# Splitting three of proj_w's seven products once more, in an attention block on one Trainium2 core

## The chip, the cores and the metric

The kernel runs on one NeuronCore of one Trainium2 chip. The time is device microseconds of one execution, from the device's own clock. A core has five engines, each with its own instruction queue that runs in order: TensorE (PE in the profile, and PEld for its weight loads), VectorE (DVE), ScalarE (ACT), GpSimd (POOL) and SyncE (SP), which here issues the DMA transfers. TensorE writes its results to PSUM, which has eight banks of 2 KB per partition; a bank holds 512 fp32 values in each of 128 partitions. VectorE and ScalarE read PSUM; GpSimd works on SBUF alone.

## The reference

The reference is one cross-attention block in fp32 over x (8 sequences of 256 tokens, width 512) and a context of the same size, 16 heads of 32:

```python
x = layer_norm(hidden_states, ln1_w, ln1_b)
q, k, v = x @ q_w + q_b, enc @ k_w + k_b, enc @ v_w + v_b      # split in 16 heads
attn = softmax(where(mask, q k^T / sqrt(32), lowest))
hidden = (attn v) @ cproj_w + cproj_b + hidden_states
y = gelu(layer_norm(hidden, ln2_w, ln2_b) @ fc_w + fc_b)         # 512 -> 2048
out = hidden + y @ proj_w + proj_b                               # 2048 -> 512
```

## The kernel before, in words

Tokens are taken in four groups of 512 (`NG` = 4, `G` = 512). First comes the attention of all groups, then, from line 1101, a loop over the groups for the two large products: the fc stage (y by fc_w, gelu) and the proj stage (h by proj_w).

Matrix products use a Strassen scheme (Winograd's form): both operands are cut in quarters 11, 12, 21, 22, sums of quarters are made (`A_SUMS` for the left operand: s3, s2, s1, s4; `B_SUMS` for the right one: t1, t2, new 12, t4), and seven products of quarters take the place of eight. The seven are listed in `FC_ORDER`: 11 by 11, 12 by 21, s2 by t2, s3 by 12, s1 by t1, s4 by 22, 22 by t4.

The fc stage applies the scheme twice: `product(k)`, k from 0 to 6, is one of the seven outer products, and its function `sub` makes one of seven inner ones, four matmuls with 128 columns each. The inner products are added up in banks by the tags f1 (two buffers), f5 (two), f6 and f7, one bank for each inner partial product, read by VectorE (`add(V, ...)`, line 1122) or ScalarE (line 1277) while TensorE fills the next. What goes to h is combined on GpSimd (`add(GP, ...)` in `made`). The weights of outer product k (fc_w's quarter and its inner sums, 1.8 MB) stand in a ring of places: `load_w2` loads the next set into the place whose product has just ended. The places are k, q and c from the attention; place v holds y2, the inner sums of y for group 0, during group 0's fc stage, and line 1365 loads a set into it in group 0's proj stage, so that from then on the ring has four places. From group 1 on, y2 has a tile of its own, tag y2, with one buffer.

The proj stage applies the scheme once: `proj(bank, a, w, first, last)` makes one of seven products as 16 matmuls of 256 columns, with proj_w's quarters and sums (`pw`, made by VectorE in group 0, a few at a time, by `some_pw`). Their order on TensorE is 11 by 11, s3 by 12, 12 by 21, s2 by t2 (the operand h21 then holds s2), s4 by 22 (h12 holds s4), s1 by t1 (h11 holds s1), 22 by t4. h's sums s3, s2, s1, s4 are made by GpSimd (`sum_h`, four pieces each, in place over quarters that are no longer read). Between the first products TensorE turns the next group's y (`turn_next`), ScalarE evicts it, and VectorE makes its sums (`sum_up(V, ys[g + 1], ...)` and `split_y`, which writes the next y2). The result is added up in `ht` (tile resm): some of it by VectorE straight from PSUM (`o_add(V, ...)`), some by GpSimd from SBUF (`o_add(GP, ...)`); `store(0)` and `store(1)` send the two halves out.

All of this is written out in the order in which each engine runs it; each engine works through its list in order, and the tile framework adds the semaphore waits. It tracks SBUF by the ranges that instructions touch, and PSUM by bank.

Of the kernel before, what the change touches and what calls it, by code (L numbers as in the profile page):

```python
# [16 lines left out]
P = 128  # L17
# [5 lines left out]
def tile_xattn_block(  # L23
# [120 lines left out]
    def place(name, at):  # L144

        return Operand(wts.tile([P, 7, HC, S], F32, tag=f"w{at}", name=name))
# [23 lines left out]
    def rows_of(t):  # L170
        return t.rearrange("p i h s -> p i (h s)")
# [16 lines left out]
    def load_w2(at):  # L188

        if not w2_order:  # L190
            return
        g, k = w2_order.pop(0)
        t = rows_of(place(f"w2_{g}_{k}", at).t)
        n = FC_ORDER[k][0]
        if n in OWN:
            load_fc_quarter(lambda i: t[:, i], n, (0, 1, 3))
            nc.sync.dma_start(t[:, 2], w2_dram[QI[n]][:, 2])
            nc.sync.dma_start(t[:, 4:7], w2_dram[QI[n]][:, 4:7])
        else:
            nc.sync.dma_start(t, w2_dram[QI[n]])  # L200
        w2[g, k], w2_place[g, k] = t, at
# [14 lines left out]
    def sum_up(eng, x, table, *which):  # L216
        for i in which:
            to, a, b, op = table[i]
            eng.tensor_tensor(x[to], x[a], x[b], op)
# [75 lines left out]
    def split_y(g, t, *which):  # L295


        y2s[g] = t

        def quarter(n):  # L300
            if n in QUARTERS:
                return ys[g].t[:, :, int(n[0]) - 1, ts(int(n[1]) - 1, P)]
            return t[:, ("t1", "t2", "t4").index(n)]

        for i in which:
            to, a, b, op = B_SUMS[i]
            nc.vector.tensor_tensor(quarter(to), quarter(a), quarter(b), op)
# [15 lines left out]
    with ExitStack() as att:  # L323
# [671 lines left out]
        def run(pieces):  # L995
            for p in pieces:
                p()
# [103 lines left out]
    with ExitStack() as mlp:  # L1101
# [16 lines left out]
        def mm(ps, lhsT, rhs, first, last):  # L1118
            nc.tensor.matmul(ps, lhsT, rhs, start=first, stop=last, skip_group_check=True)  # L1119

        def add(eng, to, a, b, op=ALU.add):
            eng.tensor_tensor(to, a, b, op)  # L1122
# [23 lines left out]

        pw_sums = sum_pw()

        def some_pw(n):
            for f in zip(range(n), pw_sums):  # L1150
                pass
# [4 lines left out]
        for g in range(NG):  # L1156
# [15 lines left out]
                    [P, 2, S], F32, tag=f"f{n}", bufs=2 if n in (1, 5) else 1, name=f"{name}_{g}"  # L1172
                )

            def sum_h(which, q):

                x = {n: h[n][:, :, 2 * q : 2 * q + 2, :] for n in h}
                to, a, b, op = {
                    "s3": ("s3", "11", "21", ALU.subtract),
                    "s2": ("21", "22", "s3", ALU.subtract),  # L1180
                    "s1": ("11", "21", "11", ALU.add),
                    "s4": ("12", "12", "21", ALU.subtract),
                }[which]
                add(GP, x[to], x[a], x[b], op)

            def load_next():
                if g + 1 < NG:
# [47 lines left out]
            def product(k, *sums):  # L1235


                wt, yn = w2[g, k], QI[FC_ORDER[k][1]]
                bank = {}

                def y_of(n):
                    if n in QUARTERS:
                        return ys[g].t[:, yn, int(n[0]) - 1, ts(int(n[1]) - 1, P)]
                    return y2s[g][:, ("t1", "t2", "t4").index(n), yn, :]

                def sub(n, w, b, first, last):
                    if first:
                        bank[n] = bank_of(n, f"pf{n}_{k}").rearrange("p i (j s) -> p (i j) s", j=2)
                    for m in range(HF // 2):
                        mm(  # L1250
                            bank[n][:, m, :],
                            wt[:, QI[w], ts(m, P)],
                            y_of(b),
                            first and m == 0,
                            last,
                        )

                def u(n):
                    return us(n, f"u{n}_{k}").rearrange("p i (j s) -> p (i j) s", j=2)

                def made(cd, n, x):
                    some_gelus()
                    if k in (3, 4) and cd != "22":
                        norm_piece()
                    if sums[0][1] is None:
                        add(V, block(sums[0][0], cd), bank[n], x)
                        return

                    r = h["s3"][:, parts[0] % 4 // 2, parts[0] % 2 * HF // 2 :][:, : HF // 2]
                    parts[0] += 1  # L1270
                    add(V, r, bank[n], x)
                    for to, base in sums:
                        add(GP, block(to, cd), block(base, cd), r)

                sub(1, "11", "11", True, False)
                u1 = u(1)
                nc.scalar.copy(u1, bank[1])  # L1277
                sub(6, "s2", "t2", True, True)
                u2 = u(2)
                add(V, u2, bank[6], u1)  # L1280
                some_gelus()
                sub(7, "s3", "12", True, False)
                u3 = u(3)
                add(V, u3, bank[7], u2)
                some_gelus()
                sub(5, "21", "t1", True, False)
                made("22", 5, u3)
                sub(1, "12", "21", False, True)
                some_gelus()
                for to, base in sums:  # L1290
                    if base:
                        add(V, block(to, "11"), bank[1], block(base, "11"))
                    else:
                        nc.scalar.copy(block(to, "11"), bank[1])
                sub(7, "22", "t4", False, True)
                made("21", 7, u2)
                sub(5, "s4", "22", False, True)
                made("12", 5, u2)
                load_w2(w2_place[g, k])
# [5 lines left out]
            gelu("11", 0)  # L1305
            ht = residual(work, hid_dram[g], "resm", f"resm_{g}")
            product(2, ("21", "21"))
            product(3, ("12", "21"))
            if g == 0:
                load_pw("11", "12", "22")  # L1310
# [25 lines left out]
            def proj(bank, a, w, first, last, tiles=(0, 1)):  # L1336
                for i in tiles:
                    for p in range(HF):
                        mm(
                            bank[:, i, :] if last_7 is None or i == 0 or bank is not last_7[0] else last_7[1],  # L1340
                            h[a][:, i, p, :],
                            pw[w][:, p, :],
                            first and p == 0 and (i == 0 or last_7 is not None and bank is last_7[0]),
                            last and p == HF - 1,
                        )
# [11 lines left out]
            def o_add(eng, b, k, x):  # L1357
                o = out_quarter(b, k)
                add(eng, o, x, o)
# [1 line left out]
            u1, u2, u3 = (us(n, f"v{n}") for n in (1, 2, 3))  # L1361
            proj(bank[1], "11", "11", True, False)
            add(V, u1, bank[1], by_tiles(projb[:, HD2:]))
            if g == 0:
                load_w2("v")
            some_gelus(HF)
            normalise_next()
            for q in range(NQF):
                sum_h("s1", q)
            proj(bank[7], "s3", "12", True, False)  # L1370
            turn_next(0)
            turn_next(1)
            some_pw(4)
            proj(bank[1], "12", "21", False, True)
            o_add(V, 0, 0, bank[1])
            for q in range(NQF):
                sum_h("s4", q)
            turn_next(2)
            turn_next(3)
            some_pw(4)  # L1380
            proj(bank[6], "21", "t2", True, True)
            add(V, u2, bank[6], u1)
            if last_7 is None:
                add(V, u3, bank[7], u2)
            else:
# [3 lines left out]
                o_add(GP, b, k, u)  # L1389
            some_pw(4)  # L1390
            bank[3] = bank_of(1, "py3")
            proj(bank[3], "12", "22", True, True)
            o_add(V, 0, 1, bank[3])
            if g + 1 < NG:
                sum_up(V, ys[g + 1], B_SUMS, 0, 1, 2, 3)
            proj(bank[5], "11", "t1", True, True)
            o_add(V, 0, 1, bank[5])
            o_add(V, 1, 1, bank[5])
            store(0)
            if g + 1 < NG:  # L1400
                y2 = wpool.tile([P, 3, 7, P], F32, tag="y2", bufs=1, name=f"y2_{g + 1}")
                split_y(g + 1, y2, 0, 1, 2, 3)
                proj(bank[7], "22", "t4", False, True)
                o_add(V, 1, 0, bank[7])
                store(1)
            else:

                store(1, slice(HD2, D))
                for i in range(2):
                    proj(bank[7], "22", "t4", False, True, (i,))  # L1410
                    o = ht[:, 2 + i, :HD2]
                    add(V, o, last_7[1] if i else bank[7][:, 0, :], o)
                    store(1, slice(HD2), (i,))
# [41 lines left out]
```

## Time and profile before

| what | us |
|---|---|
| median of 3 runs | 727.32 (727.3 to 728.82) |
| the profiled execution's own time | 727.24 |
| its span, first to last instruction | 725.1 |
| fc stage of group 0, 1 | 347.3 to 391.0, 441.7 to 485.5 |
| proj stage of group 0, 1 | 391.0 to 441.7, 485.5 to 535.6 |
| fc and proj stage of group 3 | 629.5 to 673.1, 673.1 to the end |

The span and the lines of the profile are from one profiled execution; 2.1 us of its time lie outside the span. In a timeline line stand the start, the time, the engine, the source line, the operation, written tile <- read tiles, the count, and in brackets the engine's idle time before it with what ended it. In a group line stand, after the count, the busy time of all, the mean of one in ns, and the idle time before them. A matmul in fp32 is recorded as two records. Lines 1119 and 1122 are helpers (`mm` and `add`), so groups there are told apart by their tiles: pf is fc, py is proj.

### The profile page before, as it was taken

What the parts mean: (1) busy time and instruction counts of PE and PEld (TensorE: products, weight loads), DVE (VectorE), ACT (ScalarE), POOL (GpSimd) and SP (SyncE); (2) the same over time, 40 slices, a digit from 0 to 9 for tenths busy, and PEclk for the clock granted to TensorE, in tenths of its full rate; (3) what the DMA queues carried; (4) which work ended last, traced back from release to release, by engine and by line L of the source; (5) the groups of instructions that cost most, each with busy time, mean ns of one, the idle gap of its engine ahead of it and who ended that gap; (6) DMA issues with size and microseconds to landing.
All of it is one profiled execution on the core that took longest, in us unless ns stands there. A gap on an engine that the chain in (4) does not pass through costs nothing.

```text
span 725.1 us, 14073 instructions
## 1 busy us (share of the span) xinstructions
PE 719.1 (99%) x5109; PEld 627.6 (87%) x5109; DVE 416.9 (57%) x1056; ACT 321.8 (44%) x904; POOL 501.8 (69%) x451
## 2 busy tenths in 40 slices
PE   9999999999999999999999999999999999999998
PEld 7888777887888778777999889998899988999886
DVE  4676756675456657878588576770257701666111
ACT  2277798767777778871126200244002250021500
POOL 3857799986786999876569940599305895048970
PEclk9999999999999999999999999999999999999999
DMA  9616655598648775932799603981029820182001
GB/s 301 196 60 198 213 186 207 193 327 258 203 154 292 267 261 201 367 105 88 281 407 366 266 1 136 382 314 55 1 71 390 320 105 0 59 282 83 1 0 59
DMA packets 75380, 138.83 MB, mean 191 GB/s; under 512 B 6916, under 2 KB 45104, under 8 KB 72624
## 3 DMA queue, kind: packets, MB, share of 16 engines
q1 hardware_dynamic: 75056, 137.91, 54.0%
q8 instruction: 41, 0.67, 0.4%
q14 instruction: 27, 0.22, 0.1%
q0 software_dynamic: 256, 0.02, 0.0%
HBM read 104.36 MB, written 33.55 MB: 190 GB/s over the span
## 4 chain that ended last, share of the span: by engine, by line
PE 95%; ACT 1%; issue 1%; POOL 1%; DVE 1%; DMA 1%; SPq 0%; ACTq 0%; DVEq 0%; POOLq 0%
PE py L1119 25%; PE pf L1119 23%; PE ppt L699 8%; PE pv L441 7%; PE pqT L441 7%; PE po L441 6%; PE pkT L441 5%; PE s L646 5%; PE av L715 4%; PE pkT L538 2%; PE pxt L274 1%; PE pyt L274 1%; ACT h L1221 1%; PE pct L274 1%; DMA kw<-in_L_xattn_k_w_dram 1%
## 5 line engine op out<-in xcount | busy, mean ns | idle before, releaser
L1122 POOL TENSOR_TENSOR h<-h,hs 128x512 f32<-128x512 f32 x100 | 126.7, 1291 | 120.1 <-DVE hs L1122 119.7
L1119 PEld LDWEIGHTS pf<-y,w 128*128 128x128 f32 x1568 | 175.7, 192 | 0.2
L1119 PE MATMUL pf<-y,w 128*128 128x128 f32 x1568 | 175.7, 275 | 0.0
L688 POOL TENSOR_TENSOR pr<-pr,rsum 128x512 f32<-128x512 f32 x128 | 129.5, 1045 | 35.9 <-DVE rsum L686 24.2
L674 ACT ACTIVATE pr<-pr,nmax 128x256 f32<-128x256 f32 x256 | 127.6, 501 | 35.5 <-DVE nmax L664 35.3
L664 DVE CUSTOM_DVE_ANT_0 pr<-s,mb 128x256 f32<-128x256 f32 x256 | 93.5, 413 | 39.1 <-PE s L646 27.4
L1277 ACT COPY u<-pf 128x512 f32<-128x512 f32 x28 | 16.4, 585 | 200.0 <-PE pf L1119 200.0
L1119 PE MATMUL py<-pw,h 128*128 128x256 f32 x384 | 84.9, 379 | 0.0
L1119 PE MATMUL py<-pw_t,h 128*128 128x256 f32 x384 | 84.2, 379 | 0.0
L1119 PEld LDWEIGHTS py<-pw_t,h 128*128 128x128 f32 x384 | 72.7, 190 | 9.8
L1119 PEld LDWEIGHTS py<-pw,h 128*128 128x128 f32 x384 | 72.4, 190 | 9.6
L699 PEld LDWEIGHTS ppt<-ident,pr 128*128 128x128 f32 x512 | 57.3, 140 | 14.9 <-issue 5.2
L699 PE MATMUL ppt<-ident,pr 128*128 128x128 f32 x512 | 68.8, 276 | 0.3
L1122 DVE TENSOR_TENSOR resm<-py,resm 128x512 f32<-128x512 f32 (+1 forms) x21 | 13.6, 664 | 93.6 <-PE py L1119 93.6
L1122 DVE TENSOR_TENSOR hs<-pf,u 128x512 f32<-128x512 f32 x72 | 49.5, 689 | 13.3 <-PE pf L1119 12.1
L1221 ACT ACTIVATE h<-h,cols 128x256 f32<-128x256 f32 x128 | 52.0, 494 | 10.8 <-POOL h L1122 10.8
L1122 DVE TENSOR_TENSOR u<-pf,u 128x512 f32<-128x512 f32 x56 | 38.7, 691 | 28.7 <-PE pf L1119 24.6
L704 ACT COPY pt<-ppt 128x512 f32<-128x512 f32 x96 | 51.7, 573 | 7.1 <-PE ppt L699 7.1
L441 PE MATMUL pv<-vw,ctxT 128*128 128x256 f32 x224 | 52.4, 380 | 0.0
L441 PE MATMUL pqT<-xnT,qw 128*128 128x256 f32 x224 | 51.0, 379 | 0.0
L674 ACT ACTIVATION_READ_ACCUMULATOR pr<-pr,nmax 128x1 f32 x256 | 48.7, 190 | 0.0
L441 PEld LDWEIGHTS pqT<-xnT,qw 128*128 128x128 f32 x224 | 41.4, 190 | 5.0
(145 smaller groups left out, 1040.6 us busy)
## 6 DMA issues: line engine op xcount, KB each, us to landing
w<-w_dram SPq DMA_DIRECT2D x16, 1792.0 KB, 8.9
w<-in_L_xattn_fc_w_dram SPq DMA_DIRECT2D x36, 256.0 KB, 6.1
w<-w_dram SPq DMA_DIRECT2D x12, 768.0 KB, 7.5
ctx<-in_ctx_dram SPq DMA_DIRECT2D x16, 256.0 KB, 5.0
x<-in_x_dram SPq DMA_DIRECT2D x16, 256.0 KB, 4.0
v_dram<-st_v SPq DMA_DIRECT2D x16, 256.0 KB, 2.3
v<-v_dram SPq DMA_DIRECT2D x16, 256.0 KB, 4.7
resx<-in_x_dram SPq DMA_DIRECT2D x16, 256.0 KB, 4.6
```

The lines of the kernel that those rows point to most:

```text
L274: nc.tensor.transpose(ps[:, ts(t, P)], xt[:, ts(c, P)], ident)
L441: nc.tensor.matmul(bank[n][:, i, :], l[:, c, ts(i, P)], r[:, c, :], start=first and i == 0 and c == 0, stop=last and c == HC - 1, skip_gro ...
L646: nc.tensor.matmul(banks[j][:, i, :], qT[j * HD : (j + 1) * HD, b * S + i * P : b * S + (i + 1) * P], kT[j * HD : (j + 1) * HD, b * SK : ( ...
L664: nc.vector.tensor_tensor_reduce(pr[:, j, i, :], banks[j][:, i, :], mbias[g][1][:, b, :], scale=-SCALE, scalar=FLT_MAX, op0=ALU.add, op1=A ...
L674: nc.scalar.activation(pr[:, j, i, :], pr[:, j, i, :], AF.Exp, bias=nmax[:, j, i : i + 1], scale=-1.0, accum_out=sums[:, j, i : i + 1],)
L688: nc.gpsimd.tensor_tensor(pr[:, j], pr[:, j], rsum[:, j, :, None].to_broadcast([P, NQ, SK]), ALU.mult,)
L699: nc.tensor.transpose(ps[:, kc, ts(i, P)], probs[n][:, j, i, ts(kc, P)], ident)
L704: nc.scalar.copy(pt, ps)
L715: nc.tensor.matmul(av[j * HD : (j + 1) * HD, :], vs[g, hg][:, b * NK + kc, ts(j, HD)], pts[n, j][:, kc, :], start=(kc == 0), stop=(kc == N ...
L1119: nc.tensor.matmul(ps, lhsT, rhs, start=first, stop=last, skip_group_check=True)
L1122: eng.tensor_tensor(to, a, b, op)
L1221: nc.scalar.activation(h[n][:, :, p, :], h[n][:, :, p, :], AF.Gelu_apprx_tanh, bias=col(c_fcb, half * HF + p), scale=1.0,)
```

## The change

In groups 1 to 3 (`deep`), three of the seven proj products, s2 by t2, s1 by t1 and s4 by 22, are each made by `deep_proj`: the operands are cut in quarters again and seven inner products of four matmuls with 128 columns are made. Their results go to four quarters of one bank (`ps[:, 0]` to `ps[:, 3]`), and each is read, by ScalarE or VectorE, into 128-column pieces x1, x2, x3 or of the result r.

- h's inner sums are made by VectorE: `h_blocks`, four adds for each of the three operands, into a tile `hsum` that takes turns with y2 in the one buffer of tag y2, and into pieces of s3's tile (`free`). Two of the four pieces of h's s4 sum go from GpSimd to VectorE.
- The inner sums of the three weights are made once on VectorE (`p2_sums`: t1 and 22 in group 0, t2 in group 1's fc stage). t2's and 22's share a place, and are stored to DRAM and loaded again by SP in each group (`p2_load`).
- The results of s1 by t1 and s4 by 22 are added to `ht` by GpSimd instead of VectorE.
- s1 by t1 comes ahead of s4 by 22 in all groups; the next group's y sums come one at a time within s1 by t1.
- Place v holds p2 and the pieces x1 to x3; `load_w2("v")` is gone, so the ring for fc_w keeps three places.

```diff
+        p2, p2_at = [], {"t2": 0, "22": 0, "t1": 3}
+        p2_dram = {n: tc.dram_tile([P, 3 * S * 2], F32, name=f"p2_dram_{n}") for n in ("t2", "22")}
+        def p2_place(n):
+            if not p2:
+                p2.append(rows_of(place("p2", "v").t).rearrange("p i s -> p (i s)"))
+            return p2[0][:, p2_at[n] * 2 * S :][:, : 3 * 2 * S]
...
+        def p2_sums(n):
+            sum_up(V, pw_blocks(n), B_SUMS, 0, 1, 2, 3)
+            if n != "t1":
+                nc.sync.dma_start(p2_dram[n], p2_place(n))
+        def p2_load(n):
+            nc.sync.dma_start(p2_place(n), p2_dram[n])
...
             product(2, ("21", "21"))
+            if g == 1:
+                p2_sums("t2")
...
-            if g == 0:
-                load_w2("v")
...
+            deep = g > 0
+            if deep:
+                hsum = wpool.tile([P, 3, 7, P], F32, tag="y2", bufs=1, name=f"hsum_{g}")
...
+            def h_blocks(n, s3, s2, s4, s1=None):
...
+                for to, a, b, op in A_SUMS:
+                    add(V, x["s1" if to == "21" else to], x[a], x[b], op)
+                return x
+            def deep_proj(ps, x, w, r, others=()):
+                others = iter(others)
+                ps, y = ps.rearrange("p i (j s) -> p (i j) s", j=2), pw_blocks(w)
+                x1, x2, x3 = (p2[0][:, 6 * 2 * S :][:, ts(i, P)] for i in range(3))
+                r = r.rearrange("p c s -> p (c s)").rearrange("p (b s) -> p b s", b=4)
+                def sub(i, a, b, first=False):
+                    for c in range(HF // 2):
+                        mm(ps[:, i], x[a][:, c, :], y[b][:, c, :], first and c == 0, c + 1 == HF // 2)
+                sub(0, "11", "11", True)
+                nc.scalar.copy(x1, ps[:, 0])
+                sub(1, "s2", "t2")
+                add(V, x2, ps[:, 1], x1)
+                sub(2, "s3", "12")
+                add(V, x3, ps[:, 2], x2)
+                sub(3, "s1", "t1")
+                add(V, r[:, 3], ps[:, 3], x3)
+                run(next(others, ()))
+                sub(0, "12", "21")
+                nc.scalar.copy(r[:, 0], ps[:, 0])
+                sub(2, "22", "t4")
+                add(V, r[:, 2], ps[:, 2], x2)
+                run(next(others, ()))
+                sub(3, "s4", "22")
+                add(V, r[:, 1], ps[:, 3], x2)
+                run(next(others, ()))
...
+            if deep:
+                x_s2 = h_blocks("21", *(hsum[:, i] for i in range(4)))
             proj(bank[1], "12", "21", False, True)
             o_add(V, 0, 0, bank[1])
+            if deep:
+                x_s1 = h_blocks("11", free(0), free(1), free(2))
             for q in range(NQF):
-                sum_h("s4", q)
+                sum_h("s4", q, V if deep and q % 2 else GP)
...
-            proj(bank[6], "21", "t2", True, True)
-            add(V, u2, bank[6], u1)
+            if deep:
+                deep_proj(bank[6], x_s2, "t2", hsum[:, 4])
+                p2_load("22")
+                add(V, u2, as_tiles(hsum[:, 4]), u1)
+            else:
+                proj(bank[6], "21", "t2", True, True)
+                add(V, u2, bank[6], u1)
...
-            proj(bank[3], "12", "22", True, True)
-            o_add(V, 0, 1, bank[3])
-            if g + 1 < NG:
+            if deep:
+                x_s4 = h_blocks("12", hsum[:, 0], hsum[:, 1], hsum[:, 3])
+                y_sums = []
+                if g + 1 < NG:
+                    y_sums = [lambda i=i: sum_up(V, ys[g + 1], B_SUMS, i) for i in range(4)]
+                deep_proj(bank[5], x_s1, "t1", free(3), (y_sums[:1], y_sums[1:2], y_sums[2:]))
+                for b in range(2):
+                    o_add(GP, b, 1, as_tiles(free(3)))
+                deep_proj(bank[3], x_s4, "22", hsum[:, 4])
+                if g + 1 < NG:
+                    p2_load("t2")
+                o_add(GP, 0, 1, as_tiles(hsum[:, 4]))
+            else:
+                proj(bank[5], "11", "t1", True, True)
+                o_add(V, 0, 1, bank[5])
+                o_add(V, 1, 1, bank[5])
+                p2_sums("t1")
+                proj(bank[3], "12", "22", True, True)
+                o_add(V, 0, 1, bank[3])
                 sum_up(V, ys[g + 1], B_SUMS, 0, 1, 2, 3)
...
                 split_y(g + 1, y2, 0, 1, 2, 3)
+                if not deep:
+                    p2_sums("22")
```

In the prediction, S2, S1 and S4 are the three products s2 by t2, s1 by t1 and s4 by 22, a part is one of the seven inner products of a split one, and a read is the ACT or VectorE instruction that takes a part's result from the bank.

More of the change, by code (lines that the diff above doesn't have):

```diff
@@ L1147, in tile_xattn_block, with pw_blocks @@
         pw_sums = sum_pw()
+        p2, p2_at = [], {"t2": 0, "22": 0, "t1": 3}
[4 more added lines that the diff above has]
+            return p2[0][:, p2_at[n] * 2 * S :][:, : 3 * 2 * S]
+        def pw_blocks(n):
+            x = {
+                f"{k + 1}{j + 1}": pw[n][:, k * HF // 2 : (k + 1) * HF // 2, ts(j, P)]
+                for k in range(2)
+                for j in range(2)
+            }
+            t = p2_place(n).rearrange("p (n c s) -> p n c s", n=3, c=HF // 2)
+            return x | {m: t[:, i] for i, m in enumerate(("t1", "t2", "t4"))}
+        def p2_sums(n):
[4 more added lines that the diff above has]
+            nc.sync.dma_start(p2_place(n), p2_dram[n])
         def some_pw(n):
@@ L1173, in bank_of, with sum_h @@
                 )
-            def sum_h(which, q):
+            def sum_h(which, q, eng=GP):
                 x = {n: h[n][:, :, 2 * q : 2 * q + 2, :] for n in h}
@@ L1183, in sum_h @@
                 }[which]
-                add(GP, x[to], x[a], x[b], op)
+                add(eng, x[to], x[a], x[b], op)
             def load_next():
@@ L1369, in tile_xattn_block, with free, as_tiles @@
                 sum_h("s1", q)
+            deep = g > 0
+            if deep:
+                hsum = wpool.tile([P, 3, 7, P], F32, tag="y2", bufs=1, name=f"hsum_{g}")
+                hsum = hsum.rearrange("p t n s -> p (t n s)")[:, : 5 * 2 * S]
+                hsum = hsum.rearrange("p (b c s) -> p b c s", b=5, c=HF // 2)
+            def free(i):
+                return h["s3"][:, i // 2, i % 2 * HF // 2 :][:, : HF // 2]
+            def h_blocks(n, s3, s2, s4, s1=None):
+                x = {
+                    f"{i + 1}{k + 1}": h[n][:, i, k * HF // 2 : (k + 1) * HF // 2, :]
+                    for i in range(2)
+                    for k in range(2)
+                }
+                x |= {"s3": s3, "s2": s2, "s4": s4, "s1": x["21"] if s1 is None else s1}
+                for to, a, b, op in A_SUMS:
[26 more added lines that the diff above has]
+                run(next(others, ()))
+            def as_tiles(r):
+                return r.rearrange("p c s -> p (c s)").rearrange("p (i s) -> p i s", i=2)
             proj(bank[7], "s3", "12", True, False)
@@ L1391, in tile_xattn_block @@
             bank[3] = bank_of(1, "py3")
-            proj(bank[3], "12", "22", True, True)
-            o_add(V, 0, 1, bank[3])
-            if g + 1 < NG:
+            if deep:
[17 more added lines that the diff above has]
+                o_add(V, 0, 1, bank[3])
                 sum_up(V, ys[g + 1], B_SUMS, 0, 1, 2, 3)
-            proj(bank[5], "11", "t1", True, True)
-            o_add(V, 0, 1, bank[5])
-            o_add(V, 1, 1, bank[5])
             store(0)
```

## The prediction

> **What bounds the kernel now.** I read the page's first two parts, then the chain that ended last, then the costliest groups.
>
> ```profile
> PE 719.1 (99%) x5109; PEld 627.6 (87%) x5109; DVE 416.9 (57%) x1056; ACT 321.8 (44%) x904; POOL 501.8 (69%) x451
> PEclk9999999999999999999999999999999999999999
> PE 95%; ACT 1%; issue 1%; POOL 1%; DVE 1%; DMA 1%; SPq 0%; ACTq 0%; DVEq 0%; POOLq 0%
> ```
>
> TensorE is busy 99% of the span at full granted clock, and the chain is TensorE for 95% of it. So two things move the time: TensorE's own work, and any wait that opens a gap in it. The timeline of TensorE in group 1 prices the work:
>
> ```profile
> 347.26 43.93 PE L1119 MATMUL pf<-y,w 128*128 128x128 f32 x392
> ...
> 492.39 7.07 PE L1119 MATMUL py<-pw,hs 128*128 128x256 f32 x32
> 499.30 1.04 PE L274 MATMUL pyt<-ident,hm 128*128 128x128 f32 x8
> ```
>
> A proj_w product is 32 records (16 matmuls, two passes each) of 256 columns; the next thing starts 499.30 - 492.39 = 6.91 us later, 0.216 us each. The fc stage runs 392 records of 128 columns in 43.93 us, 0.112 us each, with no gap. It can, because each of its partial products has a bank to itself while the one before is read. The timeline of VectorE there shows the reader's delay:
>
> ```profile
> 639.48 0.69 DVE L1122 TENSOR_TENSOR hs<-pf,u 128x512 f32<-128x512 f32 x1 [0.20 <-PE pf L1119]
> 640.37 0.69 DVE L1122 TENSOR_TENSOR h<-pf,h 128x512 f32<-128x512 f32 x1 [0.20 <-PE pf L1119]
> ```
>
> An eight-record part ends every 0.893 us, and the read starts 0.20 us after the slot in which the next part has already begun.
>
> **The change, part by part.**
>
> **Work taken from TensorE.** A split product is 7 parts of 4 matmuls, 56 records of 128 columns: 56 x 0.1117 = 6.25 us for 6.91. Three products in three groups: 9 x 0.66 = 5.9 us saved. That is all there is to win.
>
> **Waits put into TensorE.** All seven parts of a split product go to quarters of one bank. I looked up in the built program what each part's first matmul waits for. Of each of the six parts after the first, it is the ACT or VectorE instruction that reads the part before it, though that instruction reads another quarter of the bank. So TensorE stops, the quarter is read, TensorE starts again: 6 x 9 = 54 gaps. No row shows a 128x128 read of PSUM, so I take it from its neighbours, by lines kept apart by shape:
>
> ```profile
> L1122 DVE TENSOR_TENSOR resm<-py,resm 128x512 f32<-128x512 f32 x19 | 12.8, 690 | 88.4 <-PE py L1119 88.4
> L1122 DVE TENSOR_TENSOR resm<-py,resm 128x256 f32<-128x256 f32 x2 | 0.8, 424 | 5.2 <-PE py L1119 5.2
> L369 ACT COPY ctxT<-pct 128x256 f32<-128x256 f32 x6 | 2.2, 359 | 0.0
> L564 ACT COPY cols<-ps_cols 128x44 f32<-128x44 f32 x1 | 0.2, 195 | 2.2 <-PE ps_cols L563 2.2
> ```
>
> 690 ns for 512 columns and 424 for 256 make 1.04 ns a column, so about 290 ns for 128; ACT, between 195 and 359, about 250. The way back is in one place of the attention's end, where a matmul waits for VectorE:
>
> ```profile
> 333.87 0.69 DVE L629 TENSOR_TENSOR st_o<-po,po_u 128x512 f32<-128x512 f32 x1 [0.37 <-PE po L441]
> 334.69 1.38 PEld L441 LDWEIGHTS po<-cw,att 128*128 128x128 f32 x7 [0.41 <-DVE st_o L629]
> ```
>
> The read ends at 334.56, the weight load starts 0.13 us later (other places: 0.05 to 0.11), and the matmul behind it is recorded 0.10 us longer than its like, its own weight load no longer hidden. A gap is thus 0.20 + 0.29 + 0.09 + 0.10 = 0.68 us. Bounds: 0.20 + 0.195 + 0.05 + 0.10 = 0.55, and 0.25 + 0.42 + 0.13 + 0.10 = 0.90. I take 0.68, since both durations lie on a line through two measured sizes. 54 x 0.68 = 36.7 us (30 to 49).
>
> [...]
>
> **VectorE late for the first read.** VectorE gets 12 adds per group to make the blocks' sums, half of h's s4 sums, and 15 reads of parts. Adds of SBUF by SBUF meet POOL's. The timelines of group 0 (both at work) and group 1 (one at a time):
>
> ```profile
> 398.75 6.10 DVE L1122 TENSOR_TENSOR pw_t<-pw,pw 128x512 f32<-128x512 f32 x4
> 522.65 2.68 DVE L219 TENSOR_TENSOR y<-y 128x512 f32<-128x512 f32 x4
> 394.18 6.78 POOL L1122 TENSOR_TENSOR hs<-h,h 128x512 f32<-128x512 f32 x4
> 488.20 4.96 POOL L1122 TENSOR_TENSOR hs<-h,h 128x512 f32<-128x512 f32 x4
> 500.48 9.88 POOL L1122 TENSOR_TENSOR h<-h,h 128x512 f32<-128x512 f32 x8
> ```
>
> Alone an add takes 0.67 us on VectorE and 1.24 on POOL. Together about 1.7 on each: they take turns. Adds that read PSUM stay at 0.69. On group 1's clock:
> - S2 (h21 by t2) would start at 507.95, behind the read of bank 1 at 507.3 to 508.0 on VectorE. In VectorE's queue behind that read stand S1's four sums and two halves of s4. POOL's s1 and s4 sums (500.48 on) are themselves pushed back some 2 us by S2's four sums, so the first two adds take turns with POOL: 1.5 + 1.8 + 0.6 + 0.6 + 2 x 0.65 = 5.8, until 513.8. The second part is ready for its read at 507.95 + 0.9 + 0.68 + 0.9 + 0.2 = 510.6. TensorE waits 3.2 us more.
> - S1 follows. VectorE: last read of S2 (0.5 after S2's end), u2 and u3 (1.35), S4's four sums, three of them in turn with POOL's three adds to resm (5.5): 7.3. Due 2.7 after S2's end: 4.6 late.
> - S4: two sums of y against POOL's two adds: 1.4 late, in groups 1 and 2 only.
> Sum 3 x 7.8 + 2 x 1.4 = 26.2 us. If VectorE never met POOL it would be 1.4 + 1.8 = 3.2 a group, 9.6; if every add took 1.75, some 34. I take 26.2, since POOL's queue places its adds there.
>
> **Sums of the weights.** Four adds for t1 in group 0 lie under the 6.9 us of product 12 by 22. Four for 22, queued behind split_y, delay the first reads of group 1's fc: about 1.5 us. Four for t2, after product 2 of group 1's fc, run against POOL, some 5.5 us ahead of product 3's reads: TensorE waits about 3. Together 4.5 (0 to 7).
>
> **Costed at nothing.** The ring of three places: in group 0's fc there were three places already (the fourth held y2), each load beside as much other traffic, and the first fence shows 392 records in 43.93 us without a gap. Cover gone, each late load would stop TensorE for its lateness. Stores and loads of p2 (0.79 MB each): SP waits for S2's or S4's end before each load; behind the first stand only the second and the stores of out, and the first has all of S1 to land, the second the next 22 by t4 and fc. The deep product leaves resm to POOL, so store(0) waits for one more POOL add (1.24); the last product covers it, and split_y too: it ends some 6 us after S4, where TensorE has 6.9 of 22 by t4 and 0.9 more. The other order of S1 and S4 in group 0: t1 is made by 420.1 and would be read from 421.0.
>
> **Sum.** -5.9 + 36.7 + 26.2 + 4.5 = +61.5. The profiled execution took 727.24 us (span 725.1; median of the runs 727.32, the same): 788.7, say 789.
>
> **The rivals.**
> - *Late reads hidden.* VectorE and POOL hardly meet: -5.9 + 36.7 + 9.6 + 1 = +41, 769. Against it stands POOL's unbroken line from 488 to 510.
> - *The clock falls in the gaps.* If TensorE ran at half rate in the nine products, 9 x 6.25 = +56 more, 845. Against it, the clock row, but that has no such gaps. [...]
> - *fc_w late.* A landing at the longest seen, 16.0 us, against the 12.5 us that two products leave, is 3.5 us; at two loads a group, +21, 810.
> - *Other side: faster.* The reads lie in the shadow of the next part after all, so that the gaps vanish: 727.2 - 5.9 = 721, or with the weights' sums 726. It decides where a gap with all that comes late stays under 5.9 / 54 = 0.11 us. The read alone is over 0.19 us; only a wait list that I misread could do it.
>
> **How the numbers follow.** Forecast 0.75 (775 to 803), late reads hidden 0.14, clock 0.04, fc_w 0.04, faster 0.03. The lower bounds together give 727.2 - 5.9 + 30 + 9.6 = 761, the upper ones 727.2 - 5.9 + 49 + 34 + 7 = 811; range 760 to 811. About 0.2% (1.5 us) is what a measurement of this kernel tells from no change. Slower 0.96, same 0.01, faster 0.03.
>
> **What would show it.** Each split product should take 10.5 us or more on TensorE, with six gaps near 0.7 us named after ACT or VectorE; one gap of 3 to 5 us in S2 and in S1 of each group; TensorE's share near 92%; group 0's proj stage as long as before. Parts following each other at 0.89 us would prove me wrong, as would gaps named after DMA.

## The result, and the profile after

The changed kernel takes 801.39 us (median of 4 runs, 799.72 to 804.39) against 727.48 us for the kernel before: 1.102 times as long, with an interval of 1.098 to 1.106. The forecast was 789 us in a range of 760 to 811. The profiled execution of the changed kernel is the longest of the four, 804.39 us, with a span of 802.6; it is 77.15 us above the profiled execution of before, and this is the amount to be explained.

The page of the changed kernel, busy shares and granted clock, and the shares of the chain that ended last:

```profile
PE 748.6 (93%) x5325; PEld 651.9 (81%) x5325; DVE 484.0 (60%) x1146; ACT 326.4 (41%) x922; POOL 517.2 (64%) x454
PEclk9999999999999999999999999968999979999889
PE 77%; DVE 8%; issue 7%; POOL 4%; ACT 2%; DMA 1%; SPq 0%; DVEq 0%; POOLq 0%; ACTq 0%
```

TensorE's share fell from 99% to 93% and the chain now runs through VectorE and GpSimd too. The clock row, all nines before, has a 6, an 8, a 7 and two more 8s, all of them late in the span. TensorE's own busy time *rose* from 719.1 to 748.6 us although a split product holds less work (28 matmuls of 128 columns for 16 of 256). Two things are counted as busy that aren't work: records at half clock are longer (eight take 2.02 to 2.08 us in the timeline below), and eight records that stand alone between two gaps are counted from the start of the first to the end of the last (1.16 us, where eight within a stream take 0.893).

What TensorE waited for from 385 us to the end (total, times, longest):

```profile
PE py L1119 <- DVE p L1122: 29.0, 18, 4.7
...
PE pf L1119 <- DVE resm L1122: 2.1, 1, 2.1
PE pf L1119 <- DVE u L1122: 1.7, 1, 1.7
```

Waits named after the reads of parts, as forecast, and two in fc of group 1 (pf). No row is named after a DMA. The timeline of TensorE in group 1, from S2's third part on, then S1 and S4:

```profile
520.79 1.16 PE L1119 MATMUL py<-pw_t,hsum 128*128 128x128 f32 x8 [2.83 <-DVE p L1122]
522.34 2.02 PE L1119 MATMUL py<-p,hsum 128*128 128x128 f32 x8 [0.39 <-DVE p L1122]
...
532.23 1.16 PE L1119 MATMUL py<-p,hs 128*128 128x128 f32 x8 [0.41 <-ACT p L1435]
538.07 2.08 PE L1119 MATMUL py<-pw_t,hs 128*128 128x128 f32 x8 [4.68 <-DVE p L1122]
...
549.84 1.06 PE L1119 MATMUL py<-pw,h 128*128 128x128 f32 x8
551.30 1.16 PE L1119 MATMUL py<-p,hsum 128*128 128x128 f32 x8 [0.41 <-ACT p L1435]
552.90 1.16 PE L1119 MATMUL py<-pw,hsum 128*128 128x128 f32 x8 [0.44 <-DVE p L1122]
```

Three things stand in these lines. S4, from 549.84, is the plain case: parts start 1.46 to 1.64 us apart instead of 0.893, each after some 0.4 us of idle time. S2 and S1 each have one long wait on top, 2.83 and 4.68 us. And some parts after such a wait take 2.02 to 2.08 us for the eight records that take 1.06 to 1.16 elsewhere. Windows over S2, S1 and S4 of group 1, and last over the middle of S1 alone (start and end, length, busy time of PE, PEld, DVE, ACT and POOL, granted clock, DMA share, GB/s):

```profile
515.39:530.76 15.37, 10.51 (x58) 9.08 (x57) 6.08 (x11) 1.63 (x4) 2.06 (x2) 0.78 0.02 3
530.76:549.84 19.08, 12.27 (x59) 10.74 (x58) 8.92 (x13) 0.53 (x2) 4.60 (x3) 0.64 0.10 40
549.84:560.17 10.33, 7.81 (x58) 6.69 (x57) 3.69 (x7) 0.53 (x2) 3.22 (x2) 1.00 0.05 8
...
536.10:549.80 13.70, 10.02 (x40) 8.87 (x41) 3.98 (x8) 0.27 (x1) 0.56 (x1) 0.50 0.00 1
```

The clock, third from the end of a line, is 0.78, 0.64 and 1.00, and 0.50 in the stretch from 536.10 to 549.80. A split product without a long wait takes 10.33 us, in all three groups, and one with it 15 to 19. The nine together take 132.13 us; at 10.33 each they would be 93.0. Of the 39.2 us above that, the six long waits, each less the 0.45 us that a gap there has anyway, are 21.5 (in group 1: 2.38 in S2, 4.23 in S1); the other 17.6 are parts inside the stretches at half clock, most of which start 2.2 to 2.6 us apart.

VectorE's timeline shows what the long waits wait for. The first two lines are from S2 of group 1, the other three from S1; below them is GpSimd's line beside S1:

```profile
516.43 1.57 DVE L1122 TENSOR_TENSOR hs<-h,hs 128x512 f32<-128x512 f32 x1
...
520.45 0.28 DVE L1122 TENSOR_TENSOR p<-py,p 128x128 f32<-128x128 f32 x1
...
535.58 1.63 DVE L1122 TENSOR_TENSOR h<-hsum,h 128x512 f32<-128x512 f32 x1
537.13 0.68 DVE L1122 TENSOR_TENSOR hsum<-h,hsum 128x512 f32<-128x512 f32 x1
537.74 0.28 DVE L1122 TENSOR_TENSOR p<-py,p 128x128 f32<-128x128 f32 x1
```
```profile
532.06 4.60 POOL L1122 TENSOR_TENSOR resm<-v,resm 128x512 f32<-128x512 f32 x3 [14.60 <-DVE v L1122]
```

The 0.28 us read that TensorE waits for stands last, behind the sums for the *next* split product and, in S2, two pieces of s4. While GpSimd adds (532.06 to 536.66), an add on VectorE takes up to 1.63 us; once GpSimd is through, 0.68.

TensorE's timeline in fc of group 1:

```profile
447.20 23.33 PE L1119 MATMUL pf<-y,w 128*128 128x128 f32 x192 [2.08 <-DVE resm L1122]
472.27 20.81 PE L1119 MATMUL pf<-y,w 128*128 128x128 f32 x184 [1.74 <-DVE u L1122]
```

VectorE makes the sums of 22 (443.93 to 446.54) and of t2 (466.78 to 470.81), and then, until just before these waits end, the reads that had to queue behind them. A stretch of 3.4 us at half clock follows the first wait (447.3 to 450.7, clock 0.50). The stage takes 49.75 us for 43.77.

So the whole difference, from the profiled executions: -5.9 of TensorE work, +36.7 for the 54 gaps, +21.5 late reads, +17.6 half clock in the split products, +6.0 in group 1's fc, and +1.5 by which fc of group 0 already began later (348.73 against 347.26): 77.4 for 77.15. The last of these is in the attention, which the change doesn't touch; in a profile of the kernel before with a ring of three places (below), whose attention is the same too, that stage begins at 348.64.

### The profile page after: what moved, and what is told of

The parts are those of the page before. It is cut to its first block, busy times and chain, and to the rows that moved or that the text cites. A ratio compares the mean times of both kernels' runs of the same rounds, so it can differ in the third digit from the quotient of the medians.

```text
span 802.6 us, 14693 instructions
## 1 busy us (share of the span) xinstructions
PE 748.6 (93%) x5325; PEld 651.9 (81%) x5325; DVE 484.0 (60%) x1146; ACT 326.4 (41%) x922; POOL 517.2 (64%) x454
## 4 chain that ended last, share of the span: by engine, by line
PE 77%; DVE 8%; issue 7%; POOL 4%; ACT 2%; DMA 1%; SPq 0%; DVEq 0%; POOLq 0%; ACTq 0%
PE pf L1119 20%; PE py L1119 16%; PE ppt L699 7%; PE pv L441 6%; PE pqT L441 6%; PE po L441 5%; PE pkT L441 5%; PE s L646 4%; PE av L715 4%; POOL h L1122 2%; DVE hs L1122 2%; PE pkT L538 2%; DVE hsum L1122 2%; DMA hm<-hid_dram 1%; POOL resm L1122 1%
## 5 line engine op out<-in xcount | busy, mean ns | idle before, releaser
L1122 POOL TENSOR_TENSOR h<-h,hs 128x512 f32<-128x512 f32 x100 | 128.5, 1308 | 103.0 <-DVE hs L1122 101.3
L1119 PE MATMUL pf<-y,w 128*128 128x128 f32 x1568 | 177.9, 277 | 3.8 <-DVE resm L1122 2.1
L1119 PEld LDWEIGHTS pf<-y,w 128*128 128x128 f32 x1568 | 177.5, 193 | 4.4 <-DVE resm L1122 2.3
L664 DVE CUSTOM_DVE_ANT_0 pr<-s,mb 128x256 f32<-128x256 f32 x256 | 93.6, 414 | 39.1 <-PE s L646 27.4
L1119 PE MATMUL py<-pw,h 128*128 128x256 f32 (+1 forms) x336 | 70.2, 365 | 1.4 <-DVE hsum L1122 1.4
L1119 PEld LDWEIGHTS py<-pw,h 128*128 128x128 f32 x336 | 60.0, 190 | 9.0 <-issue 1.9
L1119 PE MATMUL py<-pw_t,h 128*128 128x256 f32 (+1 forms) x288 | 60.2, 369 | 2.9 <-DVE hsum L1122 1.4
L1119 PEld LDWEIGHTS py<-pw_t,h 128*128 128x128 f32 x288 | 52.5, 212 | 9.3 <-issue 4.4
L1122 DVE TENSOR_TENSOR hs<-pf,u 128x512 f32<-128x512 f32 x72 | 49.6, 689 | 12.9 <-PE pf L1119 11.6
L1122 POOL TENSOR_TENSOR resm<-v,resm 128x512 f32<-128x512 f32 x12 | 18.4, 1562 | 44.3 <-DVE v L1122 44.3
```

The source lines that it names most:

```text
L664: nc.vector.tensor_tensor_reduce(pr[:, j, i, :], banks[j][:, i, :], mbias[g][1][:, b, :], scale=-SCALE, scalar=FLT_MAX, op0=ALU.add, op1=A ...
```

## The experiments

My theory, after the traces: two separate faults cost nearly everything, the common bank (54 gaps) and the sums ahead of the first reads (long waits); the lowered clock is a follow-on of the long waits and not of the short gaps; the ring of three places, the stores and loads of p2, and the order cost nothing. The rivals: the short gaps lower the clock too; the reads are late from VectorE's load as such, wherever its sums stand; the transfers or the ring cost something that the gaps hide. The first two experiments remove one fault each, the third both.

**Two banks.** The parts alternate between the old bank and a second one, so that a part's neighbours in time lie elsewhere; the last two parts change places for it.

```diff
-                ps, y = ps.rearrange("p i (j s) -> p (i j) s", j=2), pw_blocks(w)
+                ps = ps.rearrange("p i (j s) -> p (i j) s", j=2)
+                odd = odd_bank.rearrange("p (b s) -> p b s", b=4)
+                ps = [ps[:, 0], odd[:, 1], ps[:, 2], odd[:, 3]]
...
-                sub(1, "s2", "t2")
+                sub(1, "s2", "t2", True)
...
+                sub(3, "s4", "22")
+                add(V, r[:, 1], ps[3], x2)
+                run(next(others, ()))
                 sub(2, "22", "t4")
...
+                odd_bank = ps_m.tile([P, G], F32, tag="mm", name=f"odd_{g}")
```

> The parts of a split product go to two banks in turn (a free bank of the transposes takes parts 1 and 3), and the last two parts change places so that neighbours never share a bank; nothing else changes. Theory (three costs: 54 gaps of 0.68 us, VectorE late for the first read of S2 and S1, clock halved after those long gaps): the short gaps go, 801.4 - 36.7 = 764.7, within 3 us; two gaps of 2 to 5 us a group stay, now ahead of part 3, and the mean granted clock stays at 0.97. Rival (VectorE's queue is the real bound, the short gaps only show it): the waits move and the time stays within 10 us of 801.

Measured: 763.41 us (761.38 to 764.93), 1.0476 times before (1.0459 to 1.0494). The waits and the timeline of TensorE with two banks:

```profile
PE odd L1119 <- DVE p L1122: 24.9, 8, 4.5
...
```
```profile
518.43 1.16 PE L1119 MATMUL odd<-p,hsum 128*128 128x128 f32 x8 [2.57 <-DVE p L1122]
519.42 1.06 PE L1119 MATMUL py<-pw_t,h 128*128 128x128 f32 x8
520.32 1.06 PE L1119 MATMUL odd<-pw_t,hsum 128*128 128x128 f32 x8
...
529.49 2.08 PE L1119 MATMUL odd<-p,h 128*128 128x128 f32 x8 [4.54 <-DVE p L1122]
531.35 1.91 PE L1119 MATMUL py<-pw_t,h 128*128 128x128 f32 x8
```

The short gaps are gone: parts follow each other at 0.89 us. The long waits have stayed, 24.9 us of eight waits against 24.2 of six in the changed kernel, and so has the half clock after most of them, but not after the 2.57 us of the first line. The medians are 801.4 - 763.4 = 38.0 us apart, the two spans 39.5. By the starts of the parts the nine products take 95.0 us for 132.1, 37.1 less: the short gaps' 36.7 are gone, the late reads cost 27.2 for 21.5, as they come due earlier without the gaps, and the half clock 11.6 for 17.6. Fc of group 1 is 1.6 us shorter, because no half clock follows its first wait here, and the rest, some 0.7, lies ahead of it. The mean clock is 0.980, a little over the 0.97 of the expectation.

**Sums later.** One bank as in the change, but the sums for S1 stand behind the reads within S2, those for S4 within S1, those of y within S4, and all of s4 is back on GpSimd.

```diff
-                x_s1 = h_blocks("11", free(0), free(1), free(2))
+                x_s1, sums_s1 = h_blocks("11", free(0), free(1), free(2))
...
-                deep_proj(bank[6], x_s2, "t2", hsum[:, 4])
+                deep_proj(bank[6], x_s2, "t2", hsum[:, 4], (sums_s1[:2], sums_s1[2:]))
...
-                deep_proj(bank[3], x_s4, "22", hsum[:, 4])
+                deep_proj(bank[3], x_s4, "22", hsum[:, 4], (y_sums[:2], y_sums[2:]))
```

> One bank as in the changed kernel, but VectorE makes S1's block sums between the reads of S2, S4's between the reads of S1, the y sums between the reads of S4, and GpSimd makes all of s4 again; the work is the same. Theory: the long gaps go, and with them the clock's falls: before 727.5 - 5.9 saved + 36.7 short gaps + 7 weight sums = 765, mean clock 0.99 or more. Rival A (the many short gaps lower the clock): clock stays near 0.97 and the time at 780 or more. Rival B (the adds only move the lateness to other reads): over 775, with gaps over 1 us ahead of later parts.

Measured: 764.84 us (762.7 to 765.47), 1.0500 (1.0483 to 1.0517). The waits with the sums later, and a window over the three split products of group 1:

```profile
PE py L1119 <- DVE p L1122: 7.5, 18, 0.5
PE py L1119 <- DVE hsum L1122: 5.6, 12, 0.5
...
```
```profile
515.15:546.18 31.03, 23.45 (x171) 20.11 (x169) 12.87 (x29) 2.70 (x8) 10.29 (x9) 1.00 0.10 29
```

The row that had 29.0 us in 18 waits has 7.5 in the same 18; the row below it is the same to the tenth in both kernels. VectorE makes as many sums for the split products as before, so in S1, where nothing else was moved, it was their place in its queue and not its load. In S2 two changes go together: the sums' place and the two pieces of s4 that went back to GpSimd (1.29 us on VectorE in the changed kernel, of the 2.4 to 4.1 us there). All 54 gaps are still there, and the clock is 1.00 over the split products of every group; the one stretch at half clock (0.998 over the span) lies in fc of group 1. So these 54 gaps of 0.35 to 0.48 us do not lower it, and the rival which has the short gaps lower the clock falls. Late reads and the clock together cost 801.4 - 764.8 = 36.6 us; the two profiled executions are 39.3 apart, and the trace of the changed kernel has 21.5 + 17.6 = 39.1.

**Both.**

> Two banks in turn and the sums between the reads, together. Theory: the three costs were all of it, apart from the weight sums: 727.5 - 5.9 + 7 = 729 (726 to 732), no gap over 0.2 us in groups 2 and 3's split products, each of them 6.3 us long. Rival (a cost of VectorE or of two engines at one bank is left): 735 or more.

The two edits above together: 728.98 us (10 runs, 726.89 to 729.98), 1.0006 (0.9995 to 1.0017), beside 728.16 for the kernel before. The waits that are left, and the timeline within S2:

```profile
PE pf L1119 <- DVE resm L1122: 2.1, 1, 2.1
PE pf L1119 <- DVE u L1122: 1.7, 1, 1.7
PE odd L1119 <- DVE p L1122: 1.1, 1, 1.1
PE py L1119 <- POOL hs L1122: 0.3, 1, 0.3
```
```profile
514.84 1.06 PE L1119 MATMUL py<-pw_t,h 128*128 128x128 f32 x8
515.73 1.06 PE L1119 MATMUL odd<-p,hsum 128*128 128x128 f32 x8
```

A split product now takes 6.25 us, S1 6.38 in groups 1 and 2 and 7.59 in group 3, where the wait of 1.1 us stands that the expectation had excluded. By the trace: -5.9, +6.0 in fc of group 1 and +1.6 in S1 make +1.7. The medians differ by 0.8, which the interval doesn't tell from nothing; four of the ten executions seem to be without the 1.6 us that half clock costs in fc (last section). With the sums mended, the second bank is worth 764.8 - 729.0 = 35.9 us, where 54 gaps of 0.68 are 36.7. The two faults explain the loss, and what the sums of the weights cost takes up the saving.

**Plain products with everything else.** From the changed kernel, with the sums where it has them, back to plain products, whose results VectorE adds again; but with all the sums, stores, loads and the three places.

```diff
-                deep_proj(bank[6], x_s2, "t2", hsum[:, 4])
+                proj(bank[6], "21", "t2", True, True)
...
-                deep_proj(bank[5], x_s1, "t1", free(3), (y_sums[:1], y_sums[1:2], y_sums[2:]))
...
-                deep_proj(bank[3], x_s4, "22", hsum[:, 4])
+                proj(bank[5], "11", "t1", True, True)
+                o_add(V, 0, 1, bank[5])
+                o_add(V, 1, 1, bank[5])
+                run(y_sums)
+                proj(bank[3], "12", "22", True, True)
...
-                o_add(GP, 0, 1, as_tiles(hsum[:, 4]))
+                o_add(V, 0, 1, bank[3])
```

> The three products are plain again in all groups, as in the kernel before, but every added sum, store and load of the change is still made (the sums in place spoil operands of the plain products, so the output isn't the reference's). Theory: what the change adds beside TensorE costs only the weight sums at the start and in group 1's fc stage: 727.5 + 7 = 735 (732 to 738). Rival (the sums, the ring of three places or p2's transfers hold up TensorE by themselves): 745 or more.

Measured: 733.46 us (730.99 to 734.23), 1.0068 (1.0048 to 1.0088). The waits, and the first wait in TensorE's timeline:

```profile
PE pf L1119 <- DVE resm L1122: 2.1, 1, 2.1
PE pf L1119 <- DVE u L1122: 1.7, 1, 1.7
PE py L1119 <- POOL hs L1122: 0.3, 1, 0.3
```
```profile
445.40 21.70 PE L1119 MATMUL pf<-y,w 128*128 128x128 f32 x192 [2.09 <-DVE resm L1122]
```

Nothing but the sums in fc of group 1 is dearer than before (the 0.3 stands in the kernel before as well). The sums of h on VectorE, the transfers of p2 and the stores add nothing that TensorE sees: from the start of group 1's proj stage to the end of the span it takes 239.7 us, the kernel before 239.6. The kernel with both edits takes 235.4 there, 4.3 less, with 1.6 of late reads in it: the split itself is worth 5.9 us. (The medians, 4.5 us apart, also hold how many executions had half clock in fc.)

**The ring alone.** The kernel before, without the fourth place.

```diff
-            if g == 0:
-                load_w2("v")
```

> The kernel before with the ring for fc_w cut to three places and nothing else. Theory (a set landing in 9 to 11 us is in time for the 12.5 that two products leave): no change, within 1 us of before, and no TensorE gap named after DMA. Rival (fc_w late): 3 us or more on top in the fc stages of groups 1 to 3.

Measured: 728.19 us (10 runs, 727.34 to 730.49), 1.0003 (0.9994 to 1.0013). No cost that can be measured, and no wait of TensorE for fc_w.

**The weights' sums spread out.** From the kernel with both edits, 22's four sums go behind the first three products of group 1's fc (two, one, one), and t2's behind its fifth and sixth (one each) and into the proj stage (two), instead of four at a time; 22's are thus no longer made in group 0.

```diff
-        def p2_sums(n):
-            sum_up(V, pw_blocks(n), B_SUMS, 0, 1, 2, 3)
+        def p2_sums(n, *which):
+            sum_up(V, pw_blocks(n), B_SUMS, *(which or (0, 1, 2, 3)))
...
             product(0, ("21", None))
+            if g == 1:
+                p2_sums("22", 0, 1)
             load_next()
             product(1, ("11", "21"))
+            if g == 1:
+                p2_sums("22", 2)
...
             product(2, ("21", "21"))
             if g == 1:
-                p2_sums("t2")
+                p2_sums("22", 3)
...
```

> Two banks and sums between the reads, and the weight sums for 22 and t2 cut up: two of 22's after product 0 of group 1's fc, one after products 1 and 2 each, t2's after products 4 and 5 and two in the proj stage. Theory: the last cost, 4.1 us of gaps and 1.8 of half clock in group 1's fc, goes, and the 5.9 us saved in the split products come out: 729.0 - 5.9 = 723 (721 to 725), faster than before. Rival (the sums hold up TensorE wherever they stand): 727 or more.

Measured: 724.80 us (5 runs, 723.91 to 726.44), 0.9956 (0.9943 to 0.9968): 3.3 us faster than the kernel before, and the only kernel here that is. The waits that are left, and the fc stage of group 1 in TensorE's timeline:

```profile
PE odd L1119 <- DVE p L1122: 1.8, 2, 1.1
PE py L1119 <- POOL hs L1122: 0.3, 1, 0.3
```
```profile
441.83 44.13 PE L1119 MATMUL pf<-y,w 128*128 128x128 f32 x392
```

The stage is 0.2 us longer than group 0's 43.93, with no wait that shows, and the clock is 1.0 over the span. Two waits of the split products remain, 0.70 in S1 of group 1 and 1.06 in S1 of group 3; by the starts of the parts they and what goes with them cost 2.4. By the trace -5.9 + 2.4 + 0.2 = -3.3, measured -3.3.

**A wait of a chosen length.** Whether a late read has a price beyond its own length was the part that my sum had at nothing. From the kernel with both edits, idle copies on VectorE after u3 hold back the first read of S1, three of them or eight.

```diff
+            if deep:
+                for _ in range(3):
+                    V.tensor_copy(as_tiles(hsum[:, 4]), bank[1])
```

> Two banks and sums between the reads, with three idle copies of a bank (0.61 us each one after another) on VectorE ahead of the first read of S1 in each of groups 1 to 3; VectorE is just in time there, so each group gets one gap of about 1.8 us. Theory: the gaps and nothing more, 729.0 + 3 x 1.8 = 734.5 (733 to 737), the clock as without the copies (0.997 to 1.0). Rival (any gap lowers the clock): 738 or more at 0.99.

> The same with eight copies: one gap of about 4.9 us a group. Theory: the gaps, 729.0 + 3 x 4.9 = 743.7, and after each a stretch at half clock that costs 2 to 4 us more: 750 to 756, clock near 0.98. Rival (the clock fell for the number of gaps, not for their length): 743 to 745 with the clock as without the copies.

Measured: with three copies 737.79 us (737.07 to 739.38), 1.0137 (1.0123 to 1.0151); with eight 750.99 (749.43 to 754.15), 1.0321 (1.0299 to 1.0343). The former lies a little over its range, the latter at its lower end. That the clock would stay as without the copies was wrong: 0.995 for 0.997. TensorE's timeline with three copies, S1 of groups 1, 2 and 3:

```profile
526.13 1.16 PE L1119 MATMUL odd<-p,h 128*128 128x128 f32 x8 [1.91 <-DVE p L1122]
527.13 1.06 PE L1119 MATMUL py<-pw_t,h 128*128 128x128 f32 x8
...
620.21 1.16 PE L1119 MATMUL odd<-p,h 128*128 128x128 f32 x8 [1.90 <-DVE p L1122]
621.21 1.58 PE L1119 MATMUL py<-pw_t,h 128*128 128x128 f32 x8
...
715.40 1.16 PE L1119 MATMUL odd<-p,h 128*128 128x128 f32 x8 [3.11 <-DVE p L1122]
716.39 1.06 PE L1119 MATMUL py<-pw_t,h 128*128 128x128 f32 x8
```

and with eight, S1 of group 1:

```profile
527.67 2.07 PE L1119 MATMUL odd<-p,h 128*128 128x128 f32 x8 [5.53 <-DVE p L1122]
529.53 1.76 PE L1119 MATMUL py<-pw_t,h 128*128 128x128 f32 x8
```

The two waits of 1.9 us are alike to 0.01 us, yet the clock falls after the second and not after the first; after 3.11 us in group 3 it doesn't fall at all. With eight copies it falls in all three waits (5.53, 5.53, 6.74), and costs 1.4 to 1.6 us each by the starts of the parts, less than the 2.5 to 2.7 of five of the six long waits in the changed kernel (4.5 in the sixth), since part of the half-clock stretch lies inside the wait: in group 1 it begins at 524.2, while the wait ends at 527.67. Against the kernel without copies S1 takes 21.6 us more in the three groups, 4.6 of them by the clock; the profiled execution has no half clock in fc of group 1, 1.6 less. That makes 20.0, and the profiled executions are 749.43 - 729.59 = 19.8 apart. With three copies S1 takes 7.8 us more, 1.6 of them by the clock, and the profiled executions are 737.68 - 729.59 = 8.1 apart.

## Why the prediction was right

The time came out 12 us above the likeliest value and inside the range, and the two leading causes were the ones forecast. By the steps of the sum:

- **Saving, -5.9.** Right: 6.25 us for a split product where no gap stands (both edits), and 5.9 us in place, by the trace of the plain products.
- **54 gaps at 0.68, +36.7.** Right: 10.33 us in S4 is 6.25 + 6 x 0.68 to the hundredth, the 128x128 read takes 0.28 to 0.29 us, and the second bank gave back 35.9 where nothing else was in the way. Taking the read's price from two other widths, and the way back from a place in the attention where a matmul waits for VectorE, was enough.
- **Late first reads, +26.2.** Mechanism right, size a little high: 21.5. S2 2.4 for 3.2 in groups 1 and 2, but 4.1 in group 3, where no transposes stand ahead of it and both first sums meet GpSimd; S1 4.2 for 4.6. S4's 1.4 did not come: only one of the two sums of y met GpSimd, they ended at 552.60, and the read that TensorE waits for was due just then.
- **Sums of the weights, +4.5.** 6.0: 2.08 for 1.5, 1.74 for 3, some 0.5 around them, and 1.6 by the clock, which the sum did not have (the plain products, without that stretch, take 48.13 us for the stage).
- **The clock, nothing in the sum.** This is the mis-sized term. I had it only as a rival of small chance, at its worst (+56); it measured 17.6 + 1.6 = 19.2 us. My reasoning stopped at the clock row of before, which "has no such gaps": I had forecast waits of 3 to 5 us myself and priced them at their length only. The profiled execution lies 15.7 us over the sum: 17.6 of clock in the products, 4.7 less of late reads, 1.5 more for the weights' sums and 1.5 in the attention make 15.9. That the time is inside the range all the same is partly luck: its upper end was made of dearer gaps, adds and weights' sums, hardly any of which came, and it happened to leave room for the clock.
- **Costed at nothing.** The ring (0.0003 of the time, within its interval), the stores and loads of p2, store(0), and the order of S1 and S4: right, by the ring alone and by the plain products. Group 0's proj stage took 50.7 us in both kernels.

The rivals: *late reads hidden* fell (21.5 us of them); *fc_w late* fell, no row names a DMA there; *faster* fell, since the parts do wait for the read of the neighbouring quarter. Whether that wait could be dropped was not tried, and no run here shows it: the tile framework sets it, since it tracks PSUM by bank. With a second bank the parts follow each other at 0.89 us. *The clock falls in the gaps* was half right: it falls, not throughout the nine products but with the long waits.

## What to carry to other kernels

Where short partial products follow each other, let neighbours write different banks: in one bank, with the waits that the framework sets there, each handover cost 0.68 us, 36 us in all here, more than six times what the split saves. Keep work for later out of the queue of the engine whose small read TensorE waits for; behind the reads of the product before, the same sums cost 1.6 us in all. And price a wait of TensorE of some 2 us or more above its length: of the 25 waits of 1.9 us or more in the kernels here, 19 brought half clock with them, at 1.4 to 4.5 us each; the same idea with both mended and the weights' sums spread out gained 3.3 of its 5.9 us.

## What was not expected of the hardware

The granted clock falls to 0.50 in stretches of 3.4, 6.8 and, once, 13.7 us. They begin at times that a wait alone does not fix, from 3.5 us before its end to 1.6 us behind it: with waits of 2.83 us and more in the changed kernel always, after 1.90 with three copies and 2.08 in fc of group 1, but not after 1.91, 2.57 or 3.11, and not with 54 gaps under 0.5. In fc of group 1 the profile of the plain products shows a full clock after the very wait (2.09 us) that lowers it in the changed kernel: the 192 records behind it take 21.70 us there and 23.33 here. With both edits the ten executions lie in two groups, 726.9 to 727.4 and 728.9 to 730.0, which would fit that one stretch of 3.4 us (1.6 us lost) being there or not. The mean granted clock on record for each agrees, 0.999 to 1.0 in the first group and 0.997 to 0.998 in the second; that the stretch lies in fc was seen only in the one that is shown here, and the groups' means are 2.2 us apart, which leaves some 0.6 open. What sets where such a stretch begins and how long it lasts, no run here shows.

VectorE's adds of SBUF by SBUF took 1.56 to 1.75 us beside GpSimd's and 0.68 alone, GpSimd's three adds 4.60 us for 3 x 1.24. Where both add without a break, in group 1 of the changed kernel, the adds end in turn: GpSimd's at 507.07, 508.74 and 510.42, VectorE's at 507.61, 509.29 and 510.97. In this kernel it reached TensorE.
